# Softmax tiles of two key tiles turned by block transposes and transfers, in a transformer block with a spline-weight MLP

## The chip, the cores and the metric

The kernel runs on one core of a Trainium2 chip. The core has five engines with queues of their own, each working through its instructions in order: TensorE (PE in the profile; PEld is its weight load), VectorE (DVE), ScalarE (ACT), GpSimd (POOL) and SyncE (SP), which here issues all transfers (DMAs). Engines wait for one another by semaphores. The metric is the device time of one execution in microseconds (us), lower is better.

## The reference

```python
xn = layernorm(x)                                 # x: 4 x 512 tokens x 512
x  = x + attention(xn) + mlp(xn)

# attention: 16 heads of 32, f32
scores = q @ k.T / sqrt(32) + slope[h] * (arange(512) - 511)   # bias goes by the key
scores = where(causal, scores, finfo.min)
attn   = softmax(scores);  ctx = attn @ v;  out = ctx @ Wo + bo

# mlp: 512 -> 2048 -> 512; the three weights are cubic splines through control points
inter = silu(xn @ gate_w.T) * (xn @ up_w.T);  out = inter @ down_w.T
```

All is float32. For the change only the softmax matters: the weights of a query tile come out with queries in the partitions and keys along the row, and the product with the values needs the keys in the partitions. So each 128x128 tile of weights has to be transposed.

## The kernel before

The kernel first does attention (up to about 410 us), then the MLP. Attention is worked through in units `(b, hg, i)`: batch row b of 4, head group hg of 4 heads (`NG = 4`, so 4 head groups a batch row, 16 in all), query tile i of 128 queries, 64 units together. Query tile i sees key tiles 0 to i, so a head group has 10 tiles of 128x128 in each of its 4 heads.

The order is written out by hand in the loop over steps n (L1013), one step to a unit, and every engine runs its instructions in that order. In step n:

- `normalize(units[n-1])` (L875): reciprocals of the sums on VectorE, then GpSimd scales the weights.
- `scores(u)` (L826): TensorE makes the scores of 4 heads in four PSUM banks (tiles 0 and 1 of a head group are made together), VectorE adds the bias `dist`, scaled by the head's slope, and finds the row's extreme (L850). There are only four such banks, so the next scores wait for these reductions.
- in every fourth step (n % 4 = 3) `values` of the head group before the current one (L901): the product of transposed weights and values.
- `exponentials(u)` on ScalarE (L866).
- `turn(old, c)` for the unit of three steps ago (`LAG = 3`) and each of its key tiles c (L885): four transposes on TensorE (L894), one for a head, into one PSUM bank of a pool of three, then one copy to the SBUF tile `pT{c}`, by VectorE for odd c (L897) and by ScalarE for even c (L899). In the order of the step, c = 0 comes ahead of the exponentials, c = 1 in their middle, c = 2 and 3 after the step's projections.
- `some_weights`: VectorE multiplies and adds that build the MLP's weights from control points, with their loads, rationed by a budget; they run out near 215 us. `items[n]` and `small[n]`: projections, layer norm of the next batch row, output projections, the stretch moments (L501), the table copies (`lay_out`, L528).

`project("k", ...)` (L770) ends with one ScalarE activation that adds the bias to kT (L795); its reader is the next head group's scores, about three steps later. `dist` is made once at the start by GpSimd (L580, L587). Buffers of the pools `soft` and `turn` are single (`bufs=1`).

Of the kernel before, what the change touches and what calls it, by code (L numbers as in the profile page):

```python
# [12 lines left out]
F32 = mybir.dt.float32  # L13
I32 = mybir.dt.int32
AF = mybir.ActivationFunctionType
ALU = mybir.AluOpType
PSUM = bass.MemoryType.PSUM

P = 128
B, S, D, H = 4, 512, 512, 16  # L20
# [3 lines left out]
NB = D // P  # L24
NTT = B * NB
NG = 4
NHG = H // NG
NEG = -3.0e38
LAG = 3
BIG = 3.4e38  # L30
# [13 lines left out]
Q32 = 32  # L44
# [352 lines left out]
def block_kernel(  # L397
# [17 lines left out]
    nc = tc.nc  # L415
# [49 lines left out]
    dist = wp.tile([P, S], F32, name="dist")  # L465
# [77 lines left out]
    with ExitStack() as att:  # L543
# [19 lines left out]
        for k in range(2):  # L563
# [16 lines left out]
        nc.gpsimd.iota(  # L580
            dist,
            pattern=[[1, S]],
            base=1 - S,
            channel_multiplier=0,
            allow_small_or_imprecise_dtypes=True,
        )
        nc.gpsimd.affine_select(  # L587
            out=dist[:, S - P :],
            in_=dist[:, S - P :],
            pattern=[[-1, P]],  # L590
            compare_op=ALU.is_ge,
            fill=NEG,
            base=0,
            channel_multiplier=1,
        )
# [174 lines left out]
        def project(name, b, hg, parts=1):  # L770
            size = S // parts
            ps = []

            def go(part=0):
# [15 lines left out]
                if name == "q":  # L790
                    nc.scalar.activation(
                        o, ps[0], AF.Identity, bias=bqs[:, g], scale=qs[:, g]
                    )
                else:
                    nc.scalar.activation(o, ps[0], AF.Identity, bias=bcol[:, 1, g])  # L795
# [28 lines left out]
        soft, pT, banks = {}, {}, {}  # L824

        def scores(u):  # L826


            b, hg, i = u
# [19 lines left out]
            for j in range(NG):  # L849
# [3 lines left out]
                    in1=dist[:, S - nk :],  # L853
# [31 lines left out]
        def turn(u, c):  # L885
# [9 lines left out]
            out = pT[b, hg, c][:, :, (i - c) * P : (i - c + 1) * P]  # L895
            if c % 2:
                nc.vector.tensor_copy(out, ps)  # L897
            else:
                nc.scalar.copy(out, ps)  # L899

        def values(b, hg):  # L901


            ps = ps_c.tile([P, S], F32, name="c")
            for c in range(NB):
                w = pT.pop((b, hg, c))
                for j in range(NG):
# [3 lines left out]
                        rhs=w[:, j, :],  # L911
# [101 lines left out]
        for n in range(len(units) + LAG):  # L1013
# [15 lines left out]
            turns = list(range(old[2] + 1)) if old else []  # L1029
# [4 lines left out]
            for c in turns[1:2]:  # L1034
                turn(old, c)
            if u and not keep_it:
                exponentials(u, range(2, NG))
            budget = 0.0 if n < NB else (2.4, 2.4, 1.2, 2.4)[n % NB] - 0.6 * len(small[n])
# [3 lines left out]
            for c in turns[2:]:  # L1042
                turn(old, c)
# [252 lines left out]
```

## Time and profile before

| | us |
|---|---|
| median of 3 runs | 563.67 (563.32 to 565.57) |
| profiled execution, span from first to last instruction | 563.4 |
| TensorE busy | 553.7 (98%) |
| VectorE busy | 355.4 (63%) |
| ScalarE busy | 295.4 (52%) |
| GpSimd busy | 184.3 (33%) |
| transposes of the softmax tiles, TensorE (L894) | 89.2, 640 instructions |
| their copies, ScalarE (L899) / VectorE (L897) | 55.2, 96 / 43.6, 64 |
| product with the values (L908) | 37.8, 512 instructions |

The profiled execution has no time of its own besides its span; the span lies 0.3 us below the median of the runs. A busy time counts overlapped instructions once for an engine; the mean duration of one matmul (278 ns for a transpose) is longer than the pace at which they follow each other. Idle time of an engine is put down to what ended it. The 16 `values` start at 59.4, 83.0, 107.3, 131.9, 168.0, 189.9, 214.9, 239.4, 270.5, 292.3, 316.7, 337.4, 361.6, 379.3, 397.8 and 408.1 us. The queue of transfers moves 36,608 packets and 75.40 MB.

### The profile page before, as it was taken

To read this page: it belongs to the slowest core of one execution; us is meant where nothing else is said; L and a number is where in the kernel's file an instruction comes from. 1 tells how busy PE (TensorE), PEld (TensorE's weight loads), DVE (VectorE), ACT (ScalarE), POOL (GpSimd) and SP (SyncE) were. 2 spreads that over 40 slices of the span, in tenths; PEclk is the share of its full clock that TensorE was granted. 3 is DMA by queue.
4 is the path that set the end of the run, shared out by engine and by line. 5 is a ranking of instruction groups with operands and counts; after the bars stand their busy time and mean duration, and the time that the engine had idled before them with its cause. 6 is when DMAs were issued, how large, how long until landed. Compare 5 with 4: busy or idle time off the path is not lost.

```text
span 563.4 us, 12222 instructions
## 1 busy us (share of the span) xinstructions
PE 553.7 (98%) x4524; PEld 297.0 (53%) x4524; DVE 355.4 (63%) x990; ACT 295.4 (52%) x782; POOL 184.3 (33%) x332
## 2 busy tenths in 40 slices
PE   7999999999999999999999999999999999999997
PEld 5645555554445554454555455554633674756652
DVE  5169998897687786465653554555633585765836
ACT  2266767655356656654665566676722262524323
POOL 2034535251325144231424144244411513323310
PEclk8999999999999999999999999999999999999999
DMA  8933337345636572133314001632334566555444
GB/s 293 352 85 74 76 78 225 75 95 142 195 104 205 179 247 82 29 95 114 101 32 146 24 1 31 208 90 48 99 101 152 171 239 216 169 174 174 172 153 163
DMA packets 36667, 76.17 MB, mean 135 GB/s; under 512 B 5920, under 2 KB 5920, under 8 KB 36096
## 3 DMA queue, kind: packets, MB, share of 16 engines
q1 hardware_dynamic: 36608, 75.40, 42.7%
q8 instruction: 35, 0.57, 0.4%
q14 instruction: 24, 0.20, 0.1%
HBM read 50.74 MB, written 23.68 MB: 132 GB/s over the span
## 4 chain that ended last, share of the span: by engine, by line
PE 86%; DVE 6%; ACT 4%; DMA 3%; issue 1%; SPq 0%; DVEq 0%
PE mm L779 17%; PE mm L894 11%; PE mm L810 9%; PE g L1070 9%; PE mm L480 7%; PE s L837 6%; PE o L1171 6%; PE c L908 5%; PE o L1117 4%; PE o L1188 3%; PE o L480 3%; ACT p L866 2%; PE mm L508 2%; DVE p L850 2%; PE o L1070 2%; PE g L1117 1%
## 5 line engine op out<-in xcount | busy, mean ns | idle before, releaser
L881 POOL TENSOR_SCALAR p<-p,inv 128x128 f32<-128x128 f32 (+3 forms) x256 | 141.9, 573 | 259.5 <-DVE inv L879 245.4
L866 ACT ACTIVATE p<-p,low 128x128 f32<-128x128 f32 (+3 forms) x256 | 140.7, 552 | 47.7 <-DVE low L850 47.5
L850 DVE CUSTOM_DVE_ANT_0 p<-s,dist 128x128 f32<-128x128 f32 (+3 forms) x256 | 109.2, 482 | 36.5 <-PE s L837 35.6
L894 PEld LDWEIGHTS mm<-ident,p 128*128 128x128 f32 x640 | 71.0, 141 | 41.0 <-issue 25.7
L894 PE MATMUL mm<-ident,p 128*128 128x128 f32 x640 | 89.2, 278 | 1.6 <-ACT pT L899 0.7
L899 ACT COPY pT<-mm 128x512 f32<-128x512 f32 x96 | 55.2, 580 | 52.9 <-PE mm L894 52.6
L1093 POOL COPY made<-inner 128x512 f32<-128x512 f32 x64 | 39.0, 633 | 98.5 <-DVE inner L1092 68.6
L1070 PE MATMUL g<-feat,wT 32*64 32x512 f32 x864 | 66.7, 592 | 0.0
L1085 ACT ACTIVATE act<-g 128x512 f32<-128x512 f32 x64 | 33.0, 603 | 57.4 <-PE g L1070 57.1
L810 PE MATMUL mm<-wv,xnT 128*128 128x512 f32 x128 | 59.5, 607 | 1.9 <-ACT xnT L764 1.9
L779 PE MATMUL mm<-xnT,wk 128*128 128x512 f32 (+1 forms) x136 | 59.3, 579 | 0.5 <-ACT xnT L764 0.2
L779 PE MATMUL mm<-xnT,wq 128*128 128x512 f32 (+1 forms) x136 | 58.0, 569 | 0.3 <-ACT pT L899 0.2
L837 PE MATMUL s<-kT,qT 32*128 32x512 f32 (+3 forms) x512 | 51.0, 468 | 0.3
L897 DVE COPY pT<-mm 128x512 f32<-128x512 f32 x64 | 43.6, 686 | 8.9 <-PE mm L894 8.4
L866 ACT ACTIVATION_READ_ACCUMULATOR p<-p,low 128x1 f32 x256 | 48.4, 189 | 0.0
L1070 PEld LDWEIGHTS g<-feat,wT 32*64 32x64 f32 x864 | 32.4, 131 | 20.0 <-issue 8.6
L1092 DVE TENSOR_TENSOR inner<-g,act 128x512 f32<-128x512 f32 x44 | 27.3, 684 | 22.8 <-PE g L1070 16.7
L480 PE MATMUL mm<-ctxT,wo 128*128 128x512 f32 x88 | 40.0, 597 | 0.0
L1171 PE MATMUL o<-inner,dRM 32*64 32x512 f32 x512 | 38.2, 588 | 0.0
L779 PEld LDWEIGHTS mm<-xnT,wk 128*128 128x128 f32 x136 | 24.5, 189 | 25.5 <-issue 21.9
L908 PE MATMUL c<-pT,v 128*32 128x128 f32 (+3 forms) x512 | 37.8, 436 | 0.0
L810 PEld LDWEIGHTS mm<-wv,xnT 128*128 128x128 f32 x128 | 23.4, 193 | 26.1 <-issue 23.8
(100 smaller groups left out, 572.5 us busy)
## 6 DMA issues: line engine op xcount, KB each, us to landing
feat<-table SPq DMA_DIRECT2D x16, 512.0 KB
inner<-made SPq DMA_DIRECT2D x32, 256.0 KB
table<-samples SPq DMA_DIRECT2D x64, 88.0 KB
xp<-in_xp_dram SPq DMA_DIRECT2D x16, 256.0 KB
samples<-xnT SPq DMA_DIRECT2D x4, 1024.0 KB
feat<-in_coef_dram SPq DMA_DIRECT2D x8, 512.0 KB
feat<-in_rowpts_dram SPq DMA_DIRECT2D x32, 128.0 KB
xt<-in_xT_dram SPq DMA_DIRECT2D x16, 256.0 KB
```

The source lines that it names most:

```text
L480: nc.tensor.matmul(ps, lhsT=wsb["o"][:, c, r * P : (r + 1) * P], rhs=ctxT[b][:, c, :], start=(c == 0), stop=(c == NB - 1),)
L779: nc.tensor.matmul(ps[0][:, tokens], lhsT=wsb[name][:, c, hg * P : (hg + 1) * P], rhs=xnT[b][:, c, tokens], start=(c == 0), stop=(c == NB ...
L810: nc.tensor.matmul(ps[0], lhsT=xnT[b][:, c, t * P : (t + 1) * P], rhs=wsb["v"][:, c, :], start=(c == 0), stop=(c == NB - 1),)
L837: nc.tensor.matmul(banks[b, hg][j][:, at : at + (k + 1) * P], lhsT=qk[b, hg, "q"][rows, k * P : (k + 1) * P], rhs=qk[b, hg, "k"][rows, : ( ...
L850: nc.vector.tensor_tensor_reduce(out=p[:, j, :nk], in0=ps[j], in1=dist[:, S - nk :], scale=-SLOPES[hg * NG + j], scalar=BIG, op0=ALU.add, ...
L866: nc.scalar.activation(p[:, j, :nk], p[:, j, :nk], AF.Exp, bias=low[:, j : j + 1], scale=-1.0, accum_out=total[:, j : j + 1],)
L881: nc.gpsimd.tensor_scalar(p[:, j, :nk], p[:, j, :nk], inv[:, j : j + 1], 1.0, ALU.mult, ALU.mult)
L894: nc.tensor.transpose(ps[:, j, :], p[:, j, c * P : (c + 1) * P], ident)
L899: nc.scalar.copy(out, ps)
L908: nc.tensor.matmul(ps[j * HD : (j + 1) * HD, c * P :], lhsT=vals[b][:, c, hg * P + j * HD : hg * P + (j + 1) * HD], rhs=w[:, j, :], start= ...
L1070: nc.tensor.matmul(ps[k][cols, :], lhsT=wT[rows, q, 2 * w + part, cols], rhs=feat[b][rows, q, part, :], start=(part == 0), stop=(part == 1),)
L1171: nc.tensor.matmul(sums[b][r][cols, :], lhsT=dR[rows, a, cols], rhs=o[rows, :], start=(a == 0), stop=False,)
```

## The change

Key tiles 1 and 3 no longer go through TensorE. For query tiles 1, 2 (key tile 1) and 3 (key tiles 1 and 3), `swap` transposes the weights of four heads in 32x32 blocks by one VectorE instruction for a key tile, from SBUF to SBUF (`blocks1` or `blocks2`), two steps after the unit's scores (`LAG_SWAP = 2`). Blocks stay in their own strip of 32 partitions; so four transfers follow, one for each strip of 32 queries. Each reads the strip's 32 partitions and writes 128 partitions of `moved`: source row y with block r becomes partition 4y + r. So that this is the key's own place, the keys of odd key tiles are stored permuted: the kT activation writes them with strides (two activations in place of one), and `dist` comes in two versions, with odd or even tiles permuted in the same way. `values` reads key tiles 1 and 3 from `moved`, in runs of 32 elements, and key tiles 0 and 2 from `pT` as before. The turns of key tile 2 now stand in the middle of the exponentials instead of after the projections. A head group has three swaps (one slot, one slot, two slots), that is 4 block transposes on VectorE instead of 4 copies there, 16 fewer transposes on TensorE, and 12 more transfers: 64 KB for one slot, 128 KB for two, in runs of 512 and 1024 bytes. `moved`, `blocks1` and `blocks2` have one buffer each; `blocks1` serves query tiles 1 and 2.

```diff
+LAG_SWAP = 2
+SLOTS = [(1, 1), (2, 1), (3, 1), (3, 3)]
...
-    dist = wp.tile([P, S], F32, name="dist")
+    dists = [wp.tile([P, S], F32, name=f"dist{k}") for k in range(2)]
...
+        for k, dist in enumerate(dists):
+            for t in range(NB):
+                part = dist[:, t * P : (t + 1) * P]
+                shape, steps = part, [[1, P]]
+                if t % 2 == k:
+                    shape = part.rearrange("p (r y) -> p r y", y=Q32)
+                    steps = [[1, NB], [NB, Q32]]
+                nc.gpsimd.iota(
+                    shape,
+                    pattern=steps,
...
+                if t == NB - 1:
+                    nc.gpsimd.affine_select(
...
-                    nc.scalar.activation(o, ps[0], AF.Identity, bias=bcol[:, 1, g])
+                    halves = lambda x: x.rearrange("p (h o m) -> p o h m", o=2, m=P)
+                    to, of = halves(o), halves(ps[0])
+                    nc.scalar.activation(to[:, 0], of[:, 0], AF.Identity, bias=bcol[:, 1, g])
+                    nc.scalar.activation(
+                        to[:, 1].rearrange("p h (r y) -> p h r y", y=Q32),
+                        of[:, 1].rearrange("p h (y r) -> p h r y", y=Q32),
+                        AF.Identity,
+                        bias=bcol[:, 1, g],
+                    )
...
-                    in1=dist[:, S - nk :],
+                    in1=dists[i % 2][:, S - nk :],
...
-            out = pT[b, hg, c][:, :, (i - c) * P : (i - c + 1) * P]
-            if c % 2:
-                nc.vector.tensor_copy(out, ps)
-            else:
-                nc.scalar.copy(out, ps)
+            nc.scalar.copy(pT[b, hg, c][:, :, (i - c) * P : (i - c + 1) * P], ps)
+
+        def swap(u):
+            b, hg, i = u
+            slots = [s for s, (of, _) in enumerate(SLOTS) if of == i]
+            if not slots:
+                return
+            if i == 1:
+                moved[b, hg] = tp.tile([P, NB, len(SLOTS), NG, Q32], F32, name="moved")
+            at = slice(slots[0], slots[-1] + 1)
+            own = tp.tile([P, NB, len(slots), NG, Q32], F32, name=f"blocks{len(slots)}")
+            for k, slot in enumerate(slots):
+                c = SLOTS[slot][1]
+                nc.vector.transpose(
+                    own[:, :, k].rearrange("p r j k -> p j r k"),
+                    soft[u][0][:, :, c * P : (c + 1) * P].rearrange("p j (r k) -> p j r k", k=Q32),
+                )
+            for a in range(NB):
+                nc.sync.dma_start(
+                    out=moved[b, hg][:, a, at].rearrange("p s j k -> p (s j k)"),
+                    in_=own[a * Q32 : (a + 1) * Q32].rearrange("p r s j k -> p r (s j k)"),
+                )
...
+            swapped = moved.pop((b, hg)).rearrange("p a s j k -> p s a j k")
             for c in range(NB):
-                w = pT.pop((b, hg, c))
+                if c % 2:
+                    slots = [s for s, (_, of) in enumerate(SLOTS) if of == c]
+                    w = swapped[:, slots[0] : slots[-1] + 1]
+                    part = lambda j: w[:, :, :, j]
+                else:
+                    w = pT.pop((b, hg, c))
+                    part = lambda j: w[:, j]
...
-                        rhs=w[:, j, :],
+                        rhs=part(j),
...
-            turns = list(range(old[2] + 1)) if old else []
+            turns = list(range(0, old[2] + 1, 2)) if old else []
             for c in turns[:1]:
                 turn(old, c)
             if u and not keep_it:
                 exponentials(u, range(2))
-            for c in turns[1:2]:
+            for c in turns[1:]:
                 turn(old, c)
             if u and not keep_it:
                 exponentials(u, range(2, NG))
+            if 0 <= n - LAG_SWAP < len(units):
+                swap(units[n - LAG_SWAP])
...
-            for c in turns[2:]:
-                turn(old, c)
```

More of the change, by code (lines that the diff above doesn't have):

```diff
@@ L575, in block_kernel @@
         nc.sync.dma_start(out=basist, in_=basis)
[L580 to L595, printed above, removed]
+        for k, dist in enumerate(dists):
[8 more added lines that the diff above has]
+                    pattern=steps,
+                    base=1 - S + t * P,
+                    channel_multiplier=0,
+                    allow_small_or_imprecise_dtypes=True,
+                )
+                if t == NB - 1:
+                    nc.gpsimd.affine_select(
+                        out=shape,
+                        in_=shape,
+                        pattern=[[-step, n] for step, n in steps],
+                        compare_op=ALU.is_ge,
+                        fill=NEG,
+                        base=0,
+                        channel_multiplier=1,
+                    )
         def row_weight_steps():
@@ L824, in block_kernel @@
         soft, pT, banks = {}, {}, {}
+        moved = {}
         def scores(u):
@@ L894, in turn @@
                 nc.tensor.transpose(ps[:, j, :], p[:, j, c * P : (c + 1) * P], ident)
-            out = pT[b, hg, c][:, :, (i - c) * P : (i - c + 1) * P]
-            if c % 2:
-                nc.vector.tensor_copy(out, ps)
-            else:
-                nc.scalar.copy(out, ps)
+            nc.scalar.copy(pT[b, hg, c][:, :, (i - c) * P : (i - c + 1) * P], ps)
[13 more added lines that the diff above has]
+                    soft[u][0][:, :, c * P : (c + 1) * P].rearrange("p j (r k) -> p j r k", k=Q32),
+                )
+            for a in range(NB):
+                nc.sync.dma_start(
+                    out=moved[b, hg][:, a, at].rearrange("p s j k -> p (s j k)"),
+                    in_=own[a * Q32 : (a + 1) * Q32].rearrange("p r s j k -> p r (s j k)"),
+                )
         def values(b, hg):
             ps = ps_c.tile([P, S], F32, name="c")
+            swapped = moved.pop((b, hg)).rearrange("p a s j k -> p s a j k")
             for c in range(NB):
-                w = pT.pop((b, hg, c))
+                if c % 2:
[5 more added lines that the diff above has]
+                    part = lambda j: w[:, j]
                 for j in range(NG):
```

## The prediction

> **What bounds the kernel now.** I read the page's busy times first, then busy time by stage, then the chain that ended last, the instructions in order of time around single steps, and at the end SyncE's queue. From the page, part 1 and three rows of part 5:
>
> ```profile
> PE 553.7 (98%) x4524; PEld 297.0 (53%) x4524; DVE 355.4 (63%) x990; ACT 295.4 (52%) x782; POOL 184.3 (33%) x332
> ...
> L894 PE MATMUL mm<-ident,p 128*128 128x128 f32 x640 | 89.2, 278 | 1.6 <-ACT pT L899 0.7 <-DVE pT L897 0.4
> L899 ACT COPY pT<-mm 128x512 f32<-128x512 f32 x96 | 55.2, 580 | 52.9 <-PE mm L894 52.6
> ...
> L897 DVE COPY pT<-mm 128x512 f32<-128x512 f32 x64 | 43.6, 686 | 8.9 <-PE mm L894 8.4
> ```
>
> TensorE is busy almost throughout, and 640 of its instructions are the transposes of the softmax tiles. The 64 copies on VectorE, and the 4 transposes ahead of each, are what goes. The mean over the span hides the stages, so next comes busy time by stretch (columns: stretch, its length, then busy us and instructions of PE, PEld, DVE, ACT, POOL, then the granted clock, the DMA share, GB/s):
>
> ```profile
> 46.00:70.00 24.00, 23.51 (x140) 12.99 (x137) 23.45 (x79) 16.82 (x51) 12.19 (x19) 1.00 0.36 87
> 70.00:94.00 24.00, 24.00 (x145) 12.90 (x143) 20.78 (x53) 15.58 (x45) 9.57 (x17) 1.00 0.53 144
> ...
> 190.00:214.00 24.00, 23.57 (x136) 12.45 (x138) 19.27 (x56) 14.59 (x42) 9.62 (x16) 1.00 0.70 229
> 214.00:238.00 24.00, 23.88 (x142) 11.45 (x141) 12.46 (x45) 14.46 (x43) 8.20 (x16) 1.00 0.15 43
> ...
> 310.00:334.00 24.00, 24.00 (x140) 12.28 (x136) 11.40 (x42) 14.14 (x42) 8.21 (x16) 1.00 0.04 14
> ```
>
> Up to about 142 us VectorE is nearly as full as TensorE (23.45 of 24 us, then some 20.8), because the weight steps run beside the softmax; after 214 us it is half idle. The clock is 1.00, so no stage is throttled. The chain agrees: it is TensorE in nearly every piece from 65 to 124 and from 215 to 360 us, VectorE at 47 to 61 us, and VectorE, a DMA and ScalarE at 124 to 141 us; at 198 to 208 us it passes through loads of the down points. So a TensorE saving counts in full only late.
>
> **What is removed.** Each of the 16 head groups loses 4 of its 10 tiles, 16 transposes. Their price is read from the order of time, not from the mean of 278 ns, which overlaps: a run of 8 transposes takes 0.93 us from its start to the next instruction (157.97 to 158.90), a run of 4 takes 0.53 (156.58 to 157.11). Query tile 1 goes from 8 to 4 transposes (0.40 saved), tile 2 from 8 and 4 to 8 (0.53), tile 3 from 8 and 8 to 8 (0.95): 1.88 us in a head group, 30 us in 16. That is the ceiling. By the busy column it would be 256 x 139 ns = 36 us, with the switches between runs counted twice.
>
> A page speaks against the change: the Trainium skill, "VectorE: DVE Perf Modes", section on the rules for kernel authors, says to transpose 128x128 on TensorE where a PSUM destination will do. Its section on the three transpose paths gives 390 ns for TensorE and 311 ns for VectorE (bf16, 32x32 blocks only); by these figures, as an estimate, 256 transposes would free 100 us of TensorE and cost 80 us of VectorE, where this trace has at most 139 ns for one on TensorE.
>
> **VectorE.** 64 copies from PSUM (686 ns each, one every 0.61) become 64 block transposes of the same 128x512 elements from SBUF. No row shows a block transpose. From below: the SBUF-to-SBUF L748, 0.46 us from start to start at its quickest. From above: twice the copy's pace, 1.2 us, if rows written in 32-float runs go at half rate. I take the copy's 0.61, the nearest row in size and type: no change in load. VectorE also stops waiting for TensorE's transposes (8.4 us in all, most of it late, where it is worth nothing).
>
> **Transfers.** Each swap is four issues on SyncE: 12 in a head group, 192 in all, 24,576 more packets and 16.8 MB. An issue is priced by the other SBUF-to-SBUF ones (from the answer for the tile `lone` and the one for line 1097; ns min/median/max, then first and last start):
>
> ```profile
> L1106 SPq DMA_DIRECT2D lone<-lone x12: 551/588/1453, 450.3 to 549.9; - x12
> L1097 SPq DMA_DIRECT2D inner<-made x32: 642/670/1585, 421.2 to 543.8; - x32
> ```
>
> So 0.59 each, between 0.33 (mid) and 0.77 (table). The round trip is shown by the one place where VectorE already waits for a transfer out of its own buffer:
>
> ```profile
> 128.67 0.68 DVE L523 COPY out<-mm 128x512 f32<-128x512 f32 x1
> 132.44 0.69 DVE L523 COPY out<-mm 64x512 f32<-64x512 f32 x1 [3.09 <-DMA moments<-out]
> ...
> 129.38 1.17 SPq L526 DMA_DIRECT2D moments<-out  x2
> ```
>
> With two issues of 1.17 us the buffer is free 3.09 us after the copy, so landing takes 1.9 us beyond the issue; with four, 2.4 + 1.9 = 4.3 us. An estimate, from these rows. By the Trainium skill, "DMA: Bandwidth & Descriptors", rules for kernel authors, transfers under 64 KB are mostly overhead, and its fixed 2.0 us (section on the anatomy of one DMA, for the other issuing path) stands beside the 1.9 us here; these are of 64 and 128 KB.
>
> **The new waits.** (a) `values` needs the landing of tile 3's swap, issued two steps earlier. At 154 us VectorE stands where that swap will be, `values` starts at 168.0: 14 us against 1.2 + 4.3. Nothing. (b) The `moved` buffer is single: the first swap of a head group waits on SyncE for `values` of the one before, in the same step. (c) `blocks1` is single: tile 2's transpose, one step later, waits for tile 1's transfers, with all later VectorE work behind it (reciprocals, score reductions, then ScalarE's exponentials). Early, between the places of the two I count 63.95 to 67.65 plus the moved transpose, 4.4 us, then 5.8 (86.7 to 92.5) and 5.2: against 4.3, hardly a stall. Late, release comes 4.3 us after `values` ends; VectorE needs 2.4 us more for the transpose and the next reductions, and TensorE asks for those banks some 12 us after `values` ends: covered. (d) SyncE. From 168 to 215 us it issues 24 table copies (18 us), some 22 loads of down tables (10 us) and 4 us of others: 32 of 47 us. With 24 swap issues (14 us) it is full, and the down loads, which already end VectorE's waits (2.4 us at 206), come later. I give these two head groups 0.5 us instead of 3.8.
>
> **Moved or split.** The kT activation becomes two halves: +0.2 to 0.35 us (256-wide exponentials go every 0.42 us, the whole kT takes 0.69), on ScalarE with 9 us idle of 24, three steps before its reader: 0. GpSimd's one iota (0.56 us) and select (0.29) become eight and two: 5.1 us at the most by these rows, ending near 8.3 us, before the first scores at 27: 0. `values` reads 32-float runs for key tiles 1 and 3: between 0 and double, which by 40% of its columns and 2.29 us a head group is 0.9 us each, 15 us in all; I take 0, since every matmul here goes by its column count. Key tile 2's turn comes ahead of the projection: the same work in a queue that is full: 0.
>
> **The end of attention.** Here nothing lies beside it:
>
> ```profile
> 402.82 2.69 POOL L881 TENSOR_SCALAR p<-p,inv 128x512 f32<-128x512 f32 x4 [2.04 <-DVE inv L879]
> ...
> 408.13 2.36 PE L908 MATMUL c<-pT,v 128*32 128x512 f32 x32
> ```
>
> GpSimd ends at 405.5; two transposes (1.3) and 4.3 us of transfer give 411.1 for the last `values`, 3.0 later than now, while TensorE has run out of turns.
>
> **Sum.** Head groups between one `values` and the next: to 59 us, VectorE bound, 0; to 83, 0.5; to 107, 1.5; to 132 (VectorE and the moments), 0.5; to 168, 1.5; to 215, 0.5 for two; to 361.6 six at 1.88, 11.3; to 398, where ScalarE's exponentials take the chain at 362 and 377, 2.0 for two; the end -3.0. Together 14.8. Some 0.6 is taken off for waits of SyncE behind table copies between 215 and 309 us: 14.2. The span of 563.4 us becomes 549.2; the median of the runs, 563.67, lies 0.3 above the span, so 549.5.
>
> **Rivals.**
> B, the ceiling: early head groups gain too, because VectorE loses its waits and transposes at 0.46 us. 30 - 3 = 27: 537. Against it: VectorE at 98% to 70 us.
> C, the block transpose takes 1.2 us: 2.4 us more VectorE work in a head group. The four up to 132 us then lose 2.4, 1.9, 0 and 1.5 instead of gaining 2.5; the next three gain 0.5 instead of 2.0 altogether; late VectorE idles and covers it; the end costs 1.2 more. 549.5 + 8.3 + 1.5 + 1.2 = 560.5. For it: only that no row shows this instruction.
> D, slower: wait (c) takes the place of the transposes. If a transfer costs SyncE 1.5 us instead of 0.59 (the rows' maxima are 1.45 and 1.59), release comes 7.9 us after the transpose. Early the gap is 4.4 to 5.8 us and VectorE has little slack: three full head groups lose 3.5, four half of that, 17.5 us; late 11.3 + 2.0 is still gained, the end costs 6: 574. It decides from about 1.1 us an issue, where the early loss eats the late gain. Against it: SyncE is idle for most of 50 to 130 us.
> E, the saving is hidden: something beside TensorE, ScalarE's chain say, holds the late steps, 563. Against it: ScalarE has 14 of 24 us.
>
> **How the numbers follow.** Chances: mine 0.50 (own range 543 to 557), B 0.10, C 0.12, D 0.22, E 0.06. What this kernel's measurement can tell from no change is about 0.5%, 560.9 to 566.5. Faster: 0.48 + 0.10 + 0.08 of C = 0.66; same: 0.02 + 0.03 + 0.05 = 0.10; slower: D and 0.02 of C and E = 0.24. The range reaches from just inside B, 538, to the middle of D, 570.
>
> **What would show it.** TensorE's L894 transposes at 384 and about 30 us less attention on its row; the queue at some 61,000 packets; stretches of a head group after 215 us shorter by 1.9 us and those before 60 us unchanged; a wait of 2 to 4 us ahead of the last `values`. C shows as the transpose's mean ns; D as VectorE idle ahead of it with the transfers of `moved` as releaser, or SyncE issues above 1.1 us. I would be wrong most easily through the price of an issue or of the transpose, which no row gives.

## The result, and the profile after

The changed kernel takes 592.03 us (median of 4 runs, 589.71 to 592.67), the kernel before 563.64 (563.32 to 565.57): a ratio of 1.049, with a 95% interval from 1.044 to 1.053. The change made the kernel slower by 28 us; 549.5 was forecast, with a range up to 570. The profiled execution took 591.6 us, its span is 589.7, 26.3 more than before.

First the page after: part 1, the chain's shares, and two rows of part 5 (busy us and mean ns of one, then the idle time ahead).

```profile
PE 546.8 (93%) x4268; PEld 275.2 (47%) x4268; DVE 351.6 (60%) x990; ACT 297.1 (50%) x798; POOL 179.6 (30%) x340
...
PE 69%; DMA 8%; DVE 8%; SPq 8%; ACT 2%; issue 2%; POOL 0%; DVEq 0%; ACTq 0%
...
L913 PE MATMUL mm<-ident,p 128*128 128x128 f32 x384 | 59.8, 295 | 1.0 <-ACT out L523 0.8
...
L928 DVE STREAM_TRANSPOSE blocks<-p 128x512 f32<-128x512 f32 x64 | 43.4, 697 | 17.3 <-DMA moved<-blocks 11.4
```

The transposes on TensorE fell from 640 to 384 and their row from 89.2 to 59.8 us, as the diff says. Yet TensorE's busy time fell by only 6.9 us and its share from 98% to 93%: it now waits, and what it does runs slower in places. SyncE's queue (SPq) stands in the chain with 8%, where before it had none.

Busy time by stretch of the kernel after, for the stretches that the prediction showed of before (the same columns):

```profile
46.00:70.00 24.00, 13.96 (x46) 6.93 (x48) 13.72 (x45) 8.32 (x24) 4.24 (x11) 0.73 0.66 160
70.00:94.00 24.00, 24.00 (x156) 11.85 (x148) 21.47 (x58) 15.80 (x46) 8.14 (x17) 0.91 0.57 137
190.00:214.00 24.00, 24.00 (x134) 11.99 (x133) 17.75 (x49) 15.46 (x45) 8.54 (x15) 1.00 0.70 211
214.00:238.00 24.00, 19.30 (x82) 9.34 (x80) 13.12 (x38) 10.82 (x31) 5.51 (x12) 0.86 0.64 206
310.00:334.00 24.00, 24.00 (x139) 11.12 (x137) 11.85 (x44) 14.10 (x42) 8.21 (x16) 1.00 0.49 139
```

Late (310 to 334) TensorE is as full as before. From 46 to 70 us TensorE and VectorE are idle for some 40% of the time, the transfer engines are busier than before (0.66 after, 0.36 before), and the granted clock is 0.73; from 214 to 238 a smaller hole of the same kind.

So the loss sits in a few places. The starts of the 16 `values` show which; each number is the time from one start to another, worked out from the order of time of each kernel's TensorE (values are counted from 1; "last to end" goes to the end of the span). The kernels to the right are experiments below.

| from value to value | before | after | no transfers | all mended | late groups, old order | two stretches |
|---|---|---|---|---|---|---|
| start to 1 | 59.4 | 69.2 | 59.9 | 59.7 | 56.5 | 59.2 |
| 1 to 4 | 72.5 | 68.8 | 66.7 | 68.8 | 72.5 | 70.3 |
| 4 to 5 | 36.1 | 42.1 | 35.3 | 41.8 | 36.2 | 36.2 |
| 5 to 6 | 21.9 | 20.1 | 20.1 | 20.1 | 21.9 | 21.9 |
| 6 to 7 | 25.0 | 31.7 | 24.8 | 30.7 | 25.1 | 25.2 |
| 7 to 9 | 55.5 | 52.3 | 53.2 | 52.3 | 54.0 | 54.0 |
| 9 to 14 | 108.9 | 101.5 | 101.4 | 101.7 | 102.3 | 101.7 |
| 14 to 16 | 28.8 | 38.1 | 27.2 | 31.1 | 32.4 | 30.7 |
| last to end | 155.3 | 166.0 | 155.6 | 156.2 | 156.3 | 155.6 |
| span | 563.4 | 589.7 | 544.2 | 562.4 | 557.0 | 554.8 |

Against before, the kernel after gains 3.7, 1.7, 3.3 and 7.5 us in four rows, 16.2 together, and loses 9.8, 6.0, 6.7, 9.3 and 10.7 in the five others, 42.5: net 26.3. The gain of a head group is there where nothing stands in its way. The five losses are five holes.

The first row holds a difference that is not the change's. The first scores, long before any swap, start at 26.86 us in the profile of before and at 24.29 in the one after; over all profiles here this start varies from 23.88 to 26.86. From the first scores to the first `values` it is 32.5 us before, 44.9 after, 33.1 without transfers and with all mended, 32.5 and 35.2 in the last two columns. So the first hole costs 12.4 us, and the spans without this difference are 28.9 apart, as the medians are (28.4).

The first hole, in order of time (start, length; in brackets the idle time ahead and what ended it):

```profile
41.45 7.53 SPq L933 DMA_DIRECT2D moved<-blocks  x8
...
49.03 0.59 SPq L622 DMA_DIRECT2D feat<-in_coef_dram  x1
49.67 1.83 SPq L625 DMA_DIRECT2D feat<-in_rowpts_dram  x4
...
56.14 1.23 DVE L639 TENSOR_TENSOR wT<-feat 128x1024 f32<-128x1024 f32 x1 [9.67 <-DMA feat<-in_rowpts_dram]
...
59.76 2.68 PE L856 MATMUL s<-kT,qT 32*128 32x384 f32 x8 [8.43 <-DVE low L869]
```

The first weight loads are issued behind the eight transfers of the first two swaps, at 49.0 us. VectorE stands 9.67 us for them, so the score reductions behind come late, and TensorE stands 8.43 us. In the kernel before the same loads were issued far ahead of their use (the third line):

```profile
19.72 0.38 SPq L612 DMA_DIRECT2D feat<-in_coef_dram  x1
20.14 4.13 SPq L615 DMA_DIRECT2D feat<-in_rowpts_dram  x4
...
47.39 1.21 DVE L629 TENSOR_TENSOR wT<-feat 128x1024 f32<-128x1024 f32 x1
```

No transfer that waits for a late VectorE result stood ahead of them there. Now the swap's transfers do, and these wait for a VectorE instruction that comes two steps after the scores. From SyncE's list of waits after (in all, times, longest):

```profile
SPq L933 <- DVE blocks L928: 93.2, 29, 23.8
```

SyncE spends 93 us standing at a swap until VectorE has made the blocks, and everything behind it in the queue stands too. Standing is not a loss in itself: before, SyncE stood 49.5 us at the stores of the stretch moments until VectorE had made them. What counts is which transfers stand behind. The clock makes the hole deeper. Stretches of 2 us after (columns as above):

```profile
56.00:58.00 2.00, 0.00 (x0) 0.00 (x0) 1.83 (x2) 0.00 (x0) 0.00 (x0) 0.50 1.06 248
58.00:60.00 2.00, 0.24 (x1) 0.24 (x2) 2.00 (x8) 0.20 (x1) 0.45 (x2) 0.50 0.37 82
60.00:62.00 2.00, 2.00 (x8) 1.28 (x8) 2.00 (x9) 2.00 (x8) 0.96 (x3) 0.50 0.00 0
62.00:64.00 2.00, 2.00 (x10) 1.57 (x8) 1.83 (x7) 1.56 (x5) 0.00 (x0) 0.50 0.34 65
```

TensorE is busy again at 60 us, but with a granted clock of 0.50 until about 64. The Trainium skill, "TensorE: Matmul & The Clock Gate", section on why this matters for your kernels, says to leave no idle gap of more than about 3 us between bursts of matmuls, since one idle window halves the clock; this trace agrees, 8.43 us of idle and 0.50 after it, but in runs further down waits of 2.46 and 2.82 us did the same, which is shorter than the page says.

The second hole (138 to 180 us) and the third (200 to 232) look alike, with the down loads: they are issued from 153.9 us (before: from 134.3), VectorE waits 6.53 us for them and TensorE 4.97 us for VectorE:

```profile
157.85 0.82 DVE L681 TENSOR_TENSOR dRM<-feat 128x640 f32<-128x640 f32 x1 [6.53 <-DMA feat<-in_downpts_dram]
...
159.39 1.80 PE L510 MATMUL mm<-xnT,stretcht 128*64 128x512 f32 x4 [4.97 <-DVE xt L489]
```

The fourth and fifth are at the end of attention. There swaps stand behind table copies in SyncE's queue, and the last swap has nothing beside it. SyncE's queue, then TensorE:

```profile
379.88 4.82 SPq L1021 DMA_DIRECT2D table<-samples  x6
384.81 2.52 SPq L933 DMA_DIRECT2D moved<-blocks  x4
387.37 7.94 SPq L1021 DMA_DIRECT2D table<-samples  x10
...
427.29 2.53 SPq L933 DMA_DIRECT2D moved<-blocks  x4
```

```profile
389.80 1.51 PE L952 MATMUL c<-moved,v 128*32 128x384 f32 x8 [3.08 <-DMA table<-samples]
...
432.20 1.51 PE L952 MATMUL c<-moved,v 128*32 128x384 f32 x8 [7.39 <-DMA moved<-blocks]
```

The prediction gave this end 3.0 us; TensorE alone waits 7.39.

### The profile page after: what moved, and what is told of

Same layout as the page of the kernel before. It is cut to its first block, busy times and chain, and to the rows that moved or that the text cites. A ratio compares the mean times of both kernels' runs of the same rounds, so it can differ in the third digit from the quotient of the medians.

```text
span 589.7 us, 12125 instructions
## 1 busy us (share of the span) xinstructions
PE 546.8 (93%) x4268; PEld 275.2 (47%) x4268; DVE 351.6 (60%) x990; ACT 297.1 (50%) x798; POOL 179.6 (30%) x340
## 3 DMA queue, kind: packets, MB, share of 16 engines
q1 hardware_dynamic: 64256, 92.19, 52.5%
## 4 chain that ended last, share of the span: by engine, by line
PE 69%; DMA 8%; DVE 8%; SPq 8%; ACT 2%; issue 2%; POOL 0%; DVEq 0%; ACTq 0%
PE mm L789 12%; PE mm L828 8%; PE g L1114 8%; PE s L856 7%; PE c L952 6%; PE mm L913 6%; PE o L1215 5%; SPq L933 5%; PE mm L482 5%; DMA moved<-blocks 3%; PE o L1161 3%; PE o L1232 3%; PE o L482 2%; DVE p L869 2%; PE o L1114 1%
## 5 line engine op out<-in xcount | busy, mean ns | idle before, releaser
L900 POOL TENSOR_SCALAR p<-p,inv 128x128 f32<-128x128 f32 (+3 forms) x256 | 135.9, 550 | 280.3 <-DVE inv L898 229.8
L869 DVE CUSTOM_DVE_ANT_0 p<-s,dist 128x128 f32<-128x128 f32 (+3 forms) x256 | 108.8, 481 | 24.5 <-PE s L856 24.3
L856 PE MATMUL s<-kT,qT 32*128 32x512 f32 (+3 forms) x512 | 61.6, 497 | 17.0 <-DVE low L869 16.8
L1137 POOL COPY made<-inner 128x512 f32<-128x512 f32 x64 | 38.9, 633 | 108.7 <-DVE inner L1136 83.7
L913 PE MATMUL mm<-ident,p 128*128 128x128 f32 x384 | 59.8, 295 | 1.0 <-ACT out L523 0.8
L789 PE MATMUL mm<-xnT,wk 128*128 128x512 f32 (+1 forms) x136 | 59.4, 579 | 0.5 <-ACT xnT L774 0.2
L913 PEld LDWEIGHTS mm<-ident,p 128*128 128x128 f32 x384 | 45.2, 149 | 29.1 <-issue 20.8
L928 DVE STREAM_TRANSPOSE blocks<-p 128x512 f32<-128x512 f32 x64 | 43.4, 697 | 17.3 <-DMA moved<-blocks 11.4
L856 PEld LDWEIGHTS s<-kT,qT 32*128 32x128 f32 x512 | 26.9, 194 | 49.2 <-DVE low L869 25.1
L1114 PEld LDWEIGHTS g<-feat,wT 32*64 32x64 f32 x864 | 30.8, 134 | 21.9 <-issue 11.1
L1215 PE MATMUL o<-inner,dRM 32*64 32x512 f32 x512 | 36.6, 588 | 0.0
L828 PEld LDWEIGHTS mm<-wv,xnT 128*128 128x128 f32 x128 | 23.6, 195 | 25.7 <-issue 24.2
```

The costliest lines, as they stand in the source:

```text
L789: nc.tensor.matmul(ps[0][:, tokens], lhsT=wsb[name][:, c, hg * P : (hg + 1) * P], rhs=xnT[b][:, c, tokens], start=(c == 0), stop=(c == NB ...
L828: nc.tensor.matmul(ps[0], lhsT=xnT[b][:, c, t * P : (t + 1) * P], rhs=wsb["v"][:, c, :], start=(c == 0), stop=(c == NB - 1),)
L856: nc.tensor.matmul(banks[b, hg][j][:, at : at + (k + 1) * P], lhsT=qk[b, hg, "q"][rows, k * P : (k + 1) * P], rhs=qk[b, hg, "k"][rows, : ( ...
L869: nc.vector.tensor_tensor_reduce(out=p[:, j, :nk], in0=ps[j], in1=dists[i % 2][:, S - nk :], scale=-SLOPES[hg * NG + j], scalar=BIG, op0=A ...
L900: nc.gpsimd.tensor_scalar(p[:, j, :nk], p[:, j, :nk], inv[:, j : j + 1], 1.0, ALU.mult, ALU.mult)
L913: nc.tensor.transpose(ps[:, j, :], p[:, j, c * P : (c + 1) * P], ident)
```

## The experiments

The theory after the first look, called Q: the time goes to the order of SyncE's queue. A swap's transfers wait there for VectorE, so loads behind them lose their head start, and swaps themselves stand behind bursts of other transfers. The rival from the prediction, called D: wait (c), the single block buffer, holds VectorE until the transfers have landed.

**The swaps' transfers issued by GpSimd.**

```diff
             for a in range(NB):
-                nc.sync.dma_start(
+                nc.gpsimd.dma_start(
```

> The changed kernel with only its 192 swap transfers issued from GpSimd's queue instead of SyncE's. Theory Q (order in SyncE's queue: the loads and table copies that it used to issue far ahead now stand behind swaps that wait for VectorE, and swaps behind bursts of table copies): SyncE runs ahead again, the four lost stretches (+9.8, +6.0, +6.7, +9.9 us between one product with the values and the next) vanish, only the wait at the end stays: about 556 us (548 to 566). Rival D (the transfers' own round trip and the wait for the single blocks buffer, my slower rival): the round trip is no shorter from another queue, 585 us or more.

Measured: 578.21 us (574.97 to 578.74), ratio 1.026 (1.023 to 1.029). It falls between the two. Three holes close all but a few us: the first `values` starts at 59.6 instead of 69.2, from the 4th to the 5th it takes 37.1 us instead of 42.1 and from the 6th to the 7th 26.7 instead of 31.7. That is what Q says, though for the second and third hole it is not the only reading: from GpSimd's queue the swaps bring the same bytes in 7,168 packets, where SyncE's queue counts 27,648 more than before. But from the 1st to the 4th it now takes 78.0 instead of 68.8: a new cost appears, since GpSimd comes to the transfers only after it has scaled the weights. VectorE's and TensorE's lists of waits in this run:

```profile
DVE blocks L928 <- DMA moved<-blocks: 24.5, 12, 4.5
```

```profile
PE c L952 <- DMA moved<-blocks: 15.2, 5, 6.9
```

VectorE's wait for the block buffer doubles from 11.4 to 24.5 us, and `values` now wait for `moved` 15.2 us, after 7.6. Changing the queue takes away about half of the loss and moves the rest.

**The first weight loads ahead of the loop.**

```diff
         load_w("o", Wo, wp)
+        for _ in range(2):
+            weights.popleft()[1]()
```

> The changed kernel with the first two weight loads (the coefficient and control point transfers of the first two spline terms) put ahead of the loop over steps, so that in SyncE's queue they stand ahead of the first swap. Nothing else is moved. Theory Q: VectorE's wait of 9.7 us at 46 us goes, and with it TensorE's slower clock after it, some 2 us: 580 us (577 to 583). Rival D: no swap's round trip changes, 592 us, the same as the changed kernel.

Measured: 583.34 us (580.59 to 586.09), ratio 1.037 (1.033 to 1.041), 8.7 below the changed kernel. The first `values` starts at 59.1, 35.2 us after the first scores, where it was 44.9: most of the first hole was the order of the queue. The 2.7 us that stay against the 32.5 of before are a wait of TensorE of 2.8 us for the score reductions. (This gain and the next ones are differences between medians of four executions each, beside runs of the kernel before that differ by up to 1.2 us. By the two ratios this one is 6.5 us, and by their 95% intervals each has some 3 us either way.)

**No transfers.** The block transposes stay, the transfers go; `values` reads a tile that is filled with zeros once, so the sums with key tiles 1 and 3 are left out.

```diff
-                moved[b, hg] = tp.tile([P, NB, len(SLOTS), NG, Q32], F32, name="moved")
+                moved[b, hg] = still
...
-            for a in range(NB):
-                nc.sync.dma_start(
-                    out=moved[b, hg][:, a, at].rearrange("p s j k -> p (s j k)"),
-                    in_=own[a * Q32 : (a + 1) * Q32].rearrange("p r s j k -> p r (s j k)"),
-                )
```

> The changed kernel without the 192 swap transfers: the block transposes run and the product with the values reads the moved buffer, which is filled with zeros once, so the weights of key tiles 1 and 3 are left out of the result. Theories Q and D agree here that everything lost comes through the transfers: 30 us of TensorE work less and no wait at the end, 536 to 546 us. If the block transposes, the strided reads of the product, the split kT activation or the moved turns cost anything of size, it is above 555.

Measured: 544.42 us (541.99 to 546.84), ratio 0.968 (0.964 to 0.972). That is within the range expected: on the engines the change is worth 18 us, and the transfers cost 47.6 (592.03 less 544.42).

**The kernel before with the transfers alone.** Its turns and copies all stay; 192 transfers of the same shapes go from a block tile to a tile that nobody reads, and a VectorE fill of one column stands for the transpose that each swap waits for.

```diff
+            nc.vector.memset(own[:, 0, 0, 0, :1], 0.0)
+            for a in range(NB):
+                nc.sync.dma_start(
+                    out=moved[:, a, at].rearrange("p s j k -> p (s j k)"),
+                    in_=own[a * Q32 : (a + 1) * Q32].rearrange("p r s j k -> p r (s j k)"),
+                )
...
+            if 0 <= n - LAG_SWAP < len(units):
+                swap(units[n - LAG_SWAP])
```

> The kernel before, with only the 192 swap transfers added at the places where the change has them, each group behind a one-element VectorE write to its source buffer; nothing reads what they bring, and TensorE's transposes all stay. Theory Q: the stalls come by the order in SyncE's queue alone, so they show here too: 563.6 plus 20 to 32, 583 to 596 us. If what costs is that the product with the values waits for the landing, there is nothing to wait for here: 564 to 569.

Measured: 595.71 us (595.21 to 596.6), ratio 1.059 (1.058 to 1.061), 33 us above before. This is the plainest of the runs: transfers whose result nobody reads cost more than the whole change. Some 30 of the 33 us lie in the places of the first four holes: from the first scores to the first `values` it takes 42.1 us (32.5 before), from the 4th to the 5th 42.6 (36.1), from the 6th to the 7th 32.1 (25.0) and from the 14th to the 16th 36.2 (28.8). In the other stretches the same transfers cost nothing: 72.5 us from the 1st to the 4th and 108.7 from the 9th to the 14th, against 72.5 and 108.9. Its order of time shows the same hole:

```profile
40.88 6.89 SPq L918 DMA_DIRECT2D moved<-blocks  x8
47.82 0.59 SPq L614 DMA_DIRECT2D feat<-in_coef_dram  x1
...
54.75 1.23 DVE L631 TENSOR_TENSOR wT<-feat 128x1024 f32<-128x1024 f32 x1 [9.48 <-DMA feat<-in_rowpts_dram]
58.37 2.67 PE L839 MATMUL s<-kT,qT 32*128 32x384 f32 x8 [6.13 <-DVE low L852]
```

VectorE waits 15.2 us for the blocks' buffer in this run too (here all three swaps share one). How much of the 33 that wait makes is not separated, but swaps stand in every stretch of attention, and the loss is in these four places alone.

**Three block slots.** Query tiles 1 and 2 no longer share a block buffer.

```diff
+        blocks = tp.tile([P, NB, 3, NG, Q32], F32, name="blocks")
...
-            own = tp.tile([P, NB, len(slots), NG, Q32], F32, name=f"blocks{len(slots)}")
+            own = blocks[:, :, {1: slice(0, 1), 2: slice(2, 3), 3: slice(0, 2)}[i]]
```

> The changed kernel with one source buffer of three slots in place of the two single ones: query tile 1 uses slot 0, tile 2 slot 2, tile 3 slots 0 and 1, so a block transpose waits for transfers of two steps before and not of one. Only this wait (c) is changed. Theory Q (order in SyncE's queue): VectorE's 11.4 us of waits for these buffers shrink and part of them was covered: 584 to 589 us. Rival D (wait (c) is what costs): most of the loss goes, 575 us or less.

Measured: 587.94 us (586.2 to 591.34), ratio 1.044 (1.040 to 1.048): 4.1 us by the medians, 2.8 by the ratios, whose intervals overlap. VectorE no longer waits for the transfers out of its block buffer (11.4 us in the changed kernel), and little comes of it. Wait (c) is there, but small; D falls as the main cause.

**The table copies issued by GpSimd.**

```diff
-                items[at].append(lambda to=to, rows=rows: nc.sync.dma_start(out=to, in_=rows))
+                items[at].append(lambda to=to, rows=rows: nc.gpsimd.dma_start(out=to, in_=rows))
```

> The changed kernel with the 96 table copies (memory to memory) issued from GpSimd's queue instead of SyncE's; swaps stay on SyncE. Theory Q: SyncE loses 72 us of issuing, swaps and down loads no longer stand behind bursts of copies: the lost stretches at 200 to 232 us and at 386 to 414 us go at least in part, 574 to 582 us. Rival D: the swaps' own round trip is what it was, 590 to 594 us.

Measured: 583.39 us (581.62 to 586.12), ratio 1.035 (1.032 to 1.039): 8.6 us, a little less than expected. From the 14th to the 16th `values` it takes 32.5 us instead of 38.1; the hole between the 6th and 7th stays (31.6). So the bursts of table copies explain most of the fourth hole and not the third.

**The last head group turned on TensorE, as before.** The diff is cut; the last group's keys also stay in their own order, and GpSimd makes the plain `dist` again for it.

```diff
-            turns = list(range(0, old[2] + 1, 2)) if old else []
+            turns = list(range(0, old[2] + 1, 1 if old and old[:2] == units[-1][:2] else 2)) if old else []
...
-            if not slots:
+            if not slots or (b, hg) == units[-1][:2]:
```

> The changed kernel with the last head group done as before the change: its odd key tiles are turned by TensorE and copied by VectorE (into the same buffer, with keys in their own order), and it has no swaps. It prices the wait at the end of attention, where the last product waited 7.4 us for the transfers, less some 1.9 us of transposes that come back; with the slower clock behind that wait 6 to 9 us: 583 to 586 us. If something else holds the end, 590 to 592.

Measured: 585.11 us (582.52 to 585.89), ratio 1.036 (1.033 to 1.040): 6.9 us, the fifth hole.

**All four mended, and the first down load one step earlier.** Only the last of these edits is shown; the others are those of the runs above.

```diff
-        weights = deque(row_weight_steps() + down_steps())
+        rows_first = row_weight_steps()
+        first, rest = down_steps()
+        rows_first.insert(len(rows_first) - 4, first)
+        weights = deque(rows_first + rest)
```

> All together: the first weight loads ahead of the loop, the first down load one spline term earlier, three block slots, table copies from GpSimd's queue, the last head group on TensorE. Theory Q: what is left is close to the run without transfers (544 us), 545 to 556 us, below the kernel before. Rival D: transfers cost what they cost, above 570 us.

Measured: 562.56 us (559.67 to 565.2), ratio 0.998 (0.996 to 1.001). The four single gains (8.7, 4.1, 8.6, 6.9) add up to 28.3, and together with the earlier down load, which has no run of its own, they gave 29.5 (by the ratios 23.6 and 28.2): as far as this resolves, they are separate. But the expectation missed. The kernel only came back to the time before; the second and third hole stayed (41.8 and 30.7 us in the table, 35.3 and 24.8 without transfers). The second now shows as the round trip of the moments, the third as down loads that take long:

```profile
153.02 0.68 DVE L525 COPY out<-mm 64x512 f32<-64x512 f32 x1 [8.53 <-DMA moments<-out]
...
206.00 0.69 DVE L681 TENSOR_TENSOR dRM<-feat 128x512 f32<-128x512 f32 x1 [3.48 <-DMA feat<-in_downpts_dram]
...
211.10 2.68 PE L860 MATMUL s<-kT,qT 32*128 32x384 f32 x8 [4.45 <-DVE low L873]
```

From 200 to 215 us the transfer engines are busy for 0.97 to 1.00 of the time in this run; before, 0.87 at the most in any 5 us there.

**The mended kernel with a quarter of the bytes or less.** As many transfers and packets, each of 128 bytes: only one head of the first slot of each swap arrives, and for the others `values` reads zeros.

```diff
-                moved[b, hg] = tp.tile([P, NB, len(SLOTS), NG, Q32], F32, name="moved")
+                moved[b, hg] = still
...
-                    out=moved[b, hg][:, a, at].rearrange("p s j k -> p (s j k)"),
-                    in_=own[a * Q32 : (a + 1) * Q32].rearrange("p r s j k -> p r (s j k)"),
+                    out=moved[b, hg][:, a, slots[0], 0],
+                    in_=own[a * Q32 : (a + 1) * Q32, :, 0, 0],
```

> The mended kernel (first loads early, three slots, table copies on GpSimd, last group on TensorE; 562.6 us) with the same number of swap transfers in the same places, each bringing only one head of its first slot, 128 bytes for 512 or 1024; the weights of the other heads of key tiles 1 and 3 are left out (zeros). It asks what holds the rest against the run without transfers (544.4): order in SyncE's queue, or the DMA engines, whose share is 0.98 at 200 to 210 us there. If order and issuing: 559 to 564 us, as the mended kernel. If the bytes on the DMA engines: the stretch at 200 to 221 us gives back some 6 us and others a little, 548 to 556.

Measured: 561.71 us (558.43 to 564.63), ratio 0.997 (0.995 to 1.000). The bytes of the swaps are not what holds the second and third hole; the number of packets and the order of issue were not separated here. In this run's profile the transfer engines are as busy (0.95 to 1.00 from 195 to 210 us), so it is other transfers, down loads and inputs of the next batch row among them, that crowd there.

**The mended kernel with the moments stored by GpSimd.**

```diff
-                    nc.sync.dma_start(out=rows[s], in_=o[half * 64 : (half + 1) * 64])
+                    nc.gpsimd.dma_start(out=rows[s], in_=o[half * 64 : (half + 1) * 64])
```

> The mended kernel with the 20 stores of the stretch moments also issued from GpSimd's queue. In the mended kernel VectorE waits 8.5 us at 144 us for these stores, which stand in SyncE's queue behind swaps and loads. If that order is what costs there, the stretch of 128 to 170 us shrinks by 4 to 6 us: 557 to 559 us. If not, 562 to 564.

Measured: 562.87 us (560.01 to 566.77), ratio 1.000 (0.997 to 1.002). No gain; the second hole is not the place of these stores in SyncE's queue alone.

**Swaps in head groups 8 to 13 only** (counted from 0, the stretch where SyncE has little to do). All other groups turn on TensorE, with plain keys, and GpSimd makes `dist` again where swapping starts and ends. The diff is cut and stands against the run with the last group on TensorE; nothing else of the mended kernel is in it.

```diff
+SWAPPED = range(8, 14)
...
-            if not slots or (b, hg) == units[-1][:2]:
+            if not slots or b * NHG + hg not in SWAPPED:
...
-            turns = list(range(0, old[2] + 1, 1 if old and old[:2] == units[-1][:2] else 2)) if old else []
+            turns = list(range(0, old[2] + 1, 2 if old and old[0] * NHG + old[1] in SWAPPED else 1)) if old else []
```

> The change for head groups 8 to 13 only, those after the weight loads and before the last burst of table copies; in the ten others TensorE turns the odd key tiles as before the change (VectorE copies them into the same buffer, keys in their own order). Table copies and loads stay on SyncE. Theory Q: where TensorE is the bound and SyncE has room, each such group gains what it gained in the changed kernel (1.1, 1.7, 1.8, 0.9, 2.0 and 0.9 us, together 8.4), and nothing is lost elsewhere: 555 us (552 to 558), below the kernel before. If the change costs wherever it stands, 563 or more.

Measured: 574.79 us (572.85 to 578.86), ratio 1.021 (1.018 to 1.024): far off. The six swapped groups gain (102.2 us from the 9th to the 14th `values`, 108.9 before). But groups without a swap lose: the 4th to the 5th takes 41.7, the 6th to the 7th 30.8. The cause is in the change's other half: all turns now stand ahead of the projections, four in a step for an unswapped group. TensorE in order of time, then stretches of 2 us, both of this run:

```profile
163.80 5.40 PE L483 MATMUL mm<-ctxT,wo 128*128 128x512 f32 x8 [2.46 <-DVE moved L940]
```

```profile
162.00:164.00 2.00, 0.20 (x1) 0.20 (x2) 2.00 (x8) 2.00 (x7) 1.26 (x3) 1.00 0.87 307
164.00:166.00 2.00, 2.00 (x4) 0.78 (x4) 0.35 (x1) 0.73 (x4) 0.00 (x0) 0.63 0.02 6
166.00:168.00 2.00, 2.00 (x4) 0.86 (x3) 0.00 (x0) 0.00 (x0) 0.00 (x0) 0.51 0.00 0
```

The projection waits 2.46 us for one of the three product banks, which VectorE empties only after its score reductions, and then runs at half clock: 5.40 us for work that takes 3.70 elsewhere in this run (170.20).

**The same, with the old order of turns for the unswapped groups.** The diff is against the run just above.

```diff
-            for c in turns[1:]:
+            late = turns[2:] if old and old[0] * NHG + old[1] not in SWAPPED else []
+            for c in turns[1 : len(turns) - len(late)]:
                 turn(old, c)
...
             for step in items[n]:
                 step()
+            for c in late:
+                turn(old, c)
```

> Head groups 8 to 13 alone are swapped, as in the run of the late groups only, and the ten others keep the order of turns that they had before (key tiles 2 and 3 behind the projections). Theory O (in that run the unswapped groups lost because all four turns were put ahead of the projections, where TensorE waited 2.5 and 3.3 us for a product bank that VectorE or ScalarE had still to empty, and ran at a clock near 0.5 for 4 us after each): the fifth, seventh and the small losses before group 8 (11.9 us in all against before) go, the six swapped groups keep their 6.7 us (group 8 to 13, 109 us before, 102.2 there), and the run comes to 556 (553 to 561), below before. Rival (the second distance tile or the copies into the moved layout cost the unswapped groups their time): it stays at 570 to 576.

Measured: 559.80 us (558.57 to 561.32), ratio 0.994 (0.992 to 0.996). Inside the range; the unswapped groups up to the 7th `values` take what they took before (72.5, 36.2, 21.9, 25.1 in the table). So the loss was the order of the turns, and the swap pays where SyncE has room: 1.5 and 6.6 us in the two rows of swapped groups. It still costs at their end: the row from the 14th to the 16th takes 3.6 us more than before, and at its start the last swapped product waits 2.31 us in a queue with table copies. Of the 6.4 us in span, 2.9 lie ahead of the first scores (23.97 us here, 26.86 before), so they belong to these two executions and not to the swaps; the remaining 3.5 fit the medians' 3.3. The gain is 0.6%, small but clear of the noise.

**Swaps in groups 0 to 2 as well, with the first loads ahead of the loop.** The diff is against the run just above and cut; `dist` is again made anew where swapping starts and ends.

```diff
-SWAPPED = range(8, 14)
+SWAPPED = (0, 1, 2, *range(8, 14))
...
         load_w("o", Wo, wp)
+        for _ in range(2):
+            weights.popleft()[1]()
```

> As the run of groups 8 to 13 with the old order, and groups 0 to 2 are swapped too, with the first two weight loads ahead of the loop. Theory O with Q (swaps pay where SyncE's queue has room, and cost where it is full): the groups 0 to 2 gain 3 to 4 us (68.8 us from the first to the fourth in the run with all mended, 72.5 before), so 2 to 4 us below the run of groups 8 to 13 with the old order: 552 to 556. Rival (swaps in the early groups push the loads of the crowded stretch behind them, and the groups from 3 on lose it again): equal to that run or above it.

Measured: 557.74 us (556.22 to 560.41), ratio 0.990 (0.987 to 0.994), 2.1 below the run before it, with intervals that overlap, and 1.7 above the range expected. The groups from 3 on lose nothing, so the rival's mechanism falls. But that swapping the early groups pays is not shown. From the 1st to the 4th `values` the profile gains 2.2 us; ahead of the 1st it loses 2.7 (35.2 us from the first scores, 32.5 in the run before it), the first wait below. At the 9th `values` this kernel is 0.6 us behind, and it gains 2.9 after it, where the two kernels do the same. This version beats both kernels: 5.3 us below the kernel before, 34 below the changed one. TensorE's two longest waits after the start show what is left (in all, times, longest):

```profile
PE s L879 <- DVE low L892: 2.8, 1, 2.8
PE c L985 <- DMA table<-samples: 2.2, 1, 2.2
```

## Why the prediction was wrong

**The saving on the engines was right.** The prediction's terms without its transfers (without the 3.0 at the end, the 0.6 for table copies, and with 3.8 instead of 0.5 for the crowded pair) would give 549.5 - 6.9 = 542.6; the run without transfers took 544.42. A swapped head group gains 1.7 us or so (22.60 instead of 24.35 between the 10th and 11th `values`), against 1.88. That the sum came so near is in part luck. Without transfers the profile gains 5.8 us from the 1st to the 4th `values`, where 2.5 were forecast; from the 5th to the 7th 1.9 instead of 3.8, and over the six groups after that 8.5 instead of 11.3. So early groups gain too, as rival B said, and late ones less.

**The unknown prices were right.** VectorE's block transpose takes 697 ns, where the copy took 686: rival C falls. An issue takes 602 ns, against 0.59; the answer for the tile `moved` of the kernel after (ns min/median/max, first and last start):

```profile
L933 SPq DMA_DIRECT2D moved<-blocks x192: 542/602/1740, 41.5 to 429.2; - x192
```

Reading in runs of 32 elements costs nothing: `values` in a free stretch takes 2.36 us, as before (304.32 to 306.68). One count was off: the queue moves 64,256 packets, not some 61,000, that is 144 for an added transfer instead of 128; the bytes are as forecast.

**The step that failed is "The new waits", (d), with "Transfers".** The prediction priced SyncE by the time its issues take, compared that with the time it had, and concluded that it was full only from 168 to 215 us. Its wait (b) even has a swap waiting on SyncE, and is charged nothing for what stands behind. What an issue costs was right; what it does to the queue was left out. SyncE's queue is in order, and a transfer that waits for VectorE holds all that stand behind it. Before, the first loads were issued from 19.7 us for use at 47.4, because nothing ahead of them waited for a late result; that head start is not seen in any busy share. The argument against D, that "SyncE is idle for most of 50 to 130 us", has the same fault: after the change it is idle because it waits. What the runs showed in its place is the lost head start: first loads issued at 49.0 us instead of 19.7, VectorE standing 9.67 us for them, TensorE 8.43 us. The transfers were charged 6.9 us in all and cost 47.6. Of these, 8.7 are the first loads, 8.6 the bursts of table copies, 6.9 the last group, 4.1 the block buffer (each by its own run, some 3 us either way), and some 18 stay, mostly in the second and third hole. With the swaps in GpSimd's queue these two nearly closed, but there both changed, the order in SyncE's queue and the number of packets (7,168 for 27,648). So what holds the two in the mended kernel, the order of issue or the number of packets, is open; the bytes of the swaps and the place of the moments' stores are excluded.

The Trainium skill has the two halves of this. "DMA: Bandwidth & Descriptors", in its section on the anatomy of one DMA, says (of the GpSimd path) that a wait on a semaphore happens on the issuing sequencer before dispatch; its rules for kernel authors say to issue a DMA early and wait for it late. The traces agree: the first loads were issued at 19.7 us before and at 49.0 after, for use at about the same step, and to issue them early again was worth 8.7 us.

**"The end of attention" was mis-sized.** 3.0 was forecast; the row "last to end" grew by 10.7, and the run with the last group on TensorE gave 6.9 back. Two transposes and one landing were counted; that these transfers stand in a queue with others was not.

**Wait (c) and rival D.** D forecast a slower kernel, 574, by the block buffer, if an issue cost more than 1.1 us. The issue costs 0.60, and three slots gave 4.1 by the medians. That the kernel got slower, as D said, came by another mechanism. B's 537 and E's 563 fall too: nothing hides the saving, the transfers undo it.

**"Moved or split"** was priced at 0. In the changed kernel itself that holds, since the run without transfers gains what was forecast. But the earlier place of the turns has a price as soon as four stand there: some 15 us between the run with late groups only and the one with the old order.

## What to carry to other kernels

Before putting a transfer that waits for a late result into a queue, list what stands behind it there and how far ahead of its use that was issued: the lost head start is the price, not the issue time. Use such a transfer where the queue has nothing urgent behind it, and keep the old path elsewhere; here swapping six of sixteen head groups gained 0.6% and nine 1%, where swapping all lost 5%. To price a change that adds transfers, add the transfers alone to the old kernel: that one run showed 33 us.

## What the runs showed of the hardware that was not expected

A wait of a few us on TensorE costs more than its length: after 8.43 us of idle the granted clock was 0.50 for 4 us of busy work, and after a wait of only 2.46 us (with hardly any matmuls in the 2 us around it) 0.63 and 0.51 for the next 4 us. In the last run a wait of 2.82 us was followed by 0.69, 0.50, 0.50 and 0.61 in the four stretches of 2 us from 56 us on. VectorE's 32x32 block transpose of 128x512 f32 from SBUF to SBUF takes 697 ns, as long as a copy of that size from PSUM.
